# An adjacency-product kernel on one core: the seventh product of layer 0 in the inner level, the bias put into PSUM banks, h normalized in its own tile

## The chip, the cores and the metric

The kernel runs on 1 core of one Trainium2 chip. The metric is the device time of one execution in microseconds (us), as the median of several runs; lower is better. A profiled execution gives, besides its own time, a trace with the start and duration of every instruction. Engines: PE is TensorE (matmuls), PEld its weight loads, DVE VectorE, ACT ScalarE, POOL GpSimd, and SP the engine whose queue issues nearly all DMAs here.

## The reference, cut to what matters

```python
x, adj                                    # (16, 1024, 512), (1024, 1024), float32
# layer 0
h = jnp.maximum(_layernorm(x, axis=-1), 0.0)
y = jnp.einsum('nm,bmd->bnd', adj, h)
x = x + jnp.einsum('bnd,do->bno', y, weight) + bias
# layer 1
h = jnp.maximum(_layernorm(x, axis=-1), 0.0)
# h = h @ W; att = softmax over j of leaky_relu(s1_i + s2_j) * adj
# x = x + elu(att @ h + beta * h)
```

Layer 0 multiplies, for each of 16 batch elements b, the adjacency matrix with h, and the result with a 512 x 512 weight matrix, adds the bias, and adds all to x. Layer 1 has the same two products, with a softmax in between.

## The kernel before

**Two-level products.** Each product of 1024 x 1024 by 1024 x 512 is done with Strassen's scheme in Winograd's form: seven products of blocks (p1 to p7) in place of eight, with sums of blocks on the way in and out (`PRODUCTS`, line 44). Each product writes into PSUM banks of a kind: Y, W or X, two banks each (one for each p, q). `ReadA` (line 125) reads finished banks into SBUF as C11, C12, C21, C22, from which the left operands S1, S2, S4 of the following weight product are made.

**The inner level.** For elements b = 1 to 15, `products_a2` (line 209) runs in layer 0. There p1, p2, p5, p6, p3 and p4 are themselves done by seven smaller products r1 to r7 (`inner_steps`, line 217). One step is two matmuls of 128x256. Step r1 writes y, r5 writes x, r4, r2 and r3 write the banks i0 and i1 of the kind, and r6 and r7 go on adding to y. ScalarE copies y out after r1 and r7 and x after r5; VectorE adds after r6, r7 and r3. Where a product is the first of its kind, x is the unused half of i0; else y and x are banks of their own:

```python
            y = bank(f"{name}_{prod}y")[:, 0:256]
            x = i0[:, 256:512] if first else bank(f"{name}_{prod}x")[:, 0:256]
```

The seventh, p7, is plain: eight matmuls of 128x512 (`plain_steps`, line 276). The products go in pairs whose steps alternate: (p1, p2), (p6, p5), (p3, p7), then p4, whose steps alternate with the first matmuls of the weight product. Each pair has seven turns. For b = 0, `products_a` (line 190) does all seven products plainly.

**The weight product.** `Weighted` (line 337) runs the seven products against the weight blocks into banks po_Y, po_X, po_W; after each, `to_residual` (line 593) adds the bank to the tile xr, which holds x and, from `add_bias` (line 585), the bias.

**What stands beside.** A plan names the work of the other engines after each turn: `after(k)` runs step k (0 to 27 in `products_a2`; `plan_out`, `plan_norm_a`, `plan_bias` and others). Engines keep the order of the program. In `plan_norm_a(b + 1)` the statistics (`Norm.sums`, line 481: two ScalarE passes over 128x512 with a sum, and a small step between) stand at steps 14 to 17 and the Relus (`relu`, line 499) at 18 and 19. `inner_left` (line 424) makes the left sums of an inner product on VectorE, four additions of 128x256. `logits` are VectorE's products with a vector.

**Buffers.** Tiles come from pools: b8 (10), b4 (12), up (7), ld (2), xp (4), b2 (5), and psum, all 8 banks of PSUM. A tile that takes a buffer waits until the last reader of the one before is done; the framework sets the semaphores, and for PSUM by whole bank. x is loaded into ld tiles (`load_x`, line 515) and normalized from there into h (b8). The inner right-hand sums `ext` (line 397) fill up, one b4 and two b2 tiles. A b4 tile `junk` takes results that nobody reads.

Of the kernel before, what the change touches and what calls it, by code (L numbers as in the profile page):

```python
# [34 lines left out]
P = 128  # L35
# [30 lines left out]
def kernel(  # L66
# [29 lines left out]
    psum = ctx.enter_context(tc.tile_pool(name="psum", bufs=8, space=bass.MemoryType.PSUM))  # L96
# [28 lines left out]
    class ReadA:  # L125
# [3 lines left out]
        def __init__(self, name, fork=None):  # L129
            self.name, self.c, self.s, self.s3_now, self.fork = name, {}, {}, True, fork  # L130

# [5 lines left out]
        def __call__(self, prod, p, ps):  # L137
            s = self.s
            if prod == "p1":
                act.copy(self.fork(p) if self.fork else self.block("C11", p), ps)  # L140
            elif prod == "p2" and self.fork:
                act.copy(self.block("C11", p), ps)
            elif prod == "p2":
                c11 = self.block("C11", p)
                add(c11, ps, c11)
            elif prod == "p6":
                act.copy(self.block("C12", p), ps)
            elif prod == "p5":
                act.copy(self.block("C22", p), ps)
            elif prod == "p7":  # L150
                c22 = self.block("C22", p)
                add(c22, ps, c22)
            elif prod == "p3":
                if not s:
                    for k in ("S1", "S2", "S4"):
                        s[k] = b4.tile([P, 2, 512], F32, tag="b4", name=f"{self.name}_{k}")
                c11, c12, c22 = (self.block(n, p) for n in ("C11", "C12", "C22"))
                s1, s2 = s["S1"][:, p, :], s["S2"][:, p, :]
                add(c12, ps, c12)
                add(s1, c12, c22)  # L160
                add(s2, s1, c11, ALU.subtract)
                if self.s3_now:
                    self.s3(p)
            else:
                act.copy(self.block("C21", p), ps)
                self.last(p)
# [23 lines left out]
    def products_a(name, a_blk, b_blk, after, products=PRODUCTS):  # L190
# [7 lines left out]
        read = ReadA(name, fork if products is FORKED else None)  # L198
# [10 lines left out]
    def products_a2(name, a_blk, b_blk, inner, weighted, after):  # L209


        read = ReadA(name)
# [4 lines left out]
        def inner_steps(prod):  # L217
# [5 lines left out]
            if first:  # L223
                banks[kind, 0], banks[kind, 1] = bank(f"{name}_{kind}0"), bank(f"{name}_{kind}1")
            i0, i1 = banks[kind, 0], banks[kind, 1]
            y = bank(f"{name}_{prod}y")[:, 0:256]
            x = i0[:, 256:512] if first else bank(f"{name}_{prod}x")[:, 0:256]
# [13 lines left out]
                "r1": (y, True), "r4": (i0[:, 0:256], first), "r5": (x, not first),  # L241
# [31 lines left out]
            order = ("r1", "r4", "r5") if first else ("r1", "r5", "r4")  # L273
            return [partial(step, r) for r in (*order, "r6", "r2", "r7", "r3")]

        def plain_steps(prod):
            _, an, bn, kind, first, last = by_name[prod]
            if first:
                banks[kind, 0], banks[kind, 1] = bank(f"{name}_{kind}0"), bank(f"{name}_{kind}1")
            return [  # L280
                partial(
                    plain_a, banks[kind, p], p, partial(a_blk, an), partial(b_blk, bn), (k,),
                    first, last,
                )
                for p in range(2) for k in range(HC)
            ]
# [5 lines left out]
        for one, two in (("p1", "p2"), ("p6", "p5")):  # L292
            ones, twos = inner_steps(one), inner_steps(two)
            turns = ones[0:2] + [t for m in range(5) for t in (twos[m], ones[m + 2])] + twos[5:]
            for m in range(7):
                turns[2 * m]()
                turns[2 * m + 1]()
                if m == 0 and k:
                    reads("p2", 0)
                    reads("p2", 1)  # L300
                elif m in (4, 5):
                    reads(one, m - 4)
                elif m == 6 and k:
                    reads(two, 0)
                    reads(two, 1)
                after(k + m)
            k += 7
        inn, pla = inner_steps("p3"), plain_steps("p7")
        turns = [(inn[0], inn[1]), pla[0:2], (inn[2], pla[2]), (inn[3], pla[3]), (inn[4], pla[4])]
        turns += [(inn[5], pla[5]), (inn[6], *pla[6:8])]  # L310
        for m, turn in enumerate(turns):
            for step in turn:
                step()
            if m == 3:
                reads("p7", 0)
            elif m == 5:
                reads("p3", 0)
            elif m == 6:
                reads("p7", 1)
                reads("p3", 1)  # L320
            after(k + m)
        k += 7
# [14 lines left out]
    class Weighted:  # L337
# [4 lines left out]

        def fork(self, kind, q, ps):
# [3 lines left out]
        def steps(self, n, left):  # L347

            prod, _, bn, kind, first, last = self.products[n]

# [34 lines left out]
    def w_sums(w):  # L385
# [9 lines left out]
        "p3": ("S4", "B22"), "p4": ("A22", "T4"),  # L395
# [3 lines left out]
    def inner_right(prod, part):  # L399

        r = adjT[INNER[prod][1]]
        if not exts:
            two = [
                pl.tile([P, 2, 2, 256], F32, tag=tag, name=f"ext_{i}")
                for i, (pl, tag) in enumerate(((up, "up"),) * 7 + ((b4, "b4"),))
            ]
            one = [b2.tile([P, 2, 256], F32, tag="b2", name=f"ext_{i}") for i in (8, 9)]
            ext = [two[i // 2][:, i % 2] for i in range(16)] + one
# [28 lines left out]
    def layer0_a2(b, plan):  # L437
        beside(plan)(-1)

        class Inner(dict):  # L440
# [5 lines left out]
        lefts[b] = products_a2(  # L446
            f"y{b}", lambda n, k: h_blk(b, n)[:, k, :], lambda n, k: adjT[n][:, k, :],
            Inner(), weighted[b], beside(plan),
        )
# [15 lines left out]
    class Norm:  # L465


        def __init__(self, name, src, dst, junk=None):
            self.name, self.src, self.dst, self.junk = name, src, dst, junk
# [11 lines left out]
        def sums(self, k):  # L481
# [5 lines left out]
            junk = self.dst[:, k, :] if self.junk is None else self.junk  # L487
# [11 lines left out]
        def relu(self, c=slice(None)):  # L499
            for k in range(self.n):  # L500
                act.activation(
                    self.dst[:, k, c], self.src[:, k, c], AF.Relu,
# [9 lines left out]
    xs = {}  # L512
    h_norms = {}

    def load_x(b, k, pl=None, tag="ld"):
        t = (pl or ld).tile([P, 2, D], F32, tag=tag, name=f"x_{b}_{k}")
        sp.dma_start(out=t, in_=x[b, ts(k, 2 * P), :].rearrange("(k p) d -> p k d", p=P))
        xs[b, k] = t

    def h_stats(b, k, c=0):  # L520

        if c == 0:
            if k % 2 == 0:
                hs[b, k // 2] = b8.tile([P, HC, D], F32, tag="b8", name=f"h_{b}_{k // 2}")
            dst = hs[b, k // 2][:, ts(k % 2, 2), :]
            h_norms[b, k] = Norm(f"h{b}_{k}", xs.pop((b, k)), dst)
# [40 lines left out]
    def layer0_a(b, plan):  # L567
        beside(plan)(-1)
        lefts[b] = products_a(
            f"y{b}", lambda n, k: h_blk(b, n)[:, k, :], lambda n, k: adjT[n][:, k, :],  # L570
            beside(plan),
# [13 lines left out]
    def add_bias(b, nh, q, oh):  # L585

        t = xrs[b, nh, q][:, :, ts(oh, HD)]
        bias = bias_bc[:, None, ts(oh, HD)].to_broadcast([P, 2, HD])
        pool.tensor_tensor(t, t, bias, op=ALU.add)
# [12 lines left out]
    def layer0_b(b, plan):  # L602
        left = lefts.pop(b)
        if b in weighted:
            weighted.pop(b).rest(1, left, beside(plan))
        else:
            Weighted(f"po{b}", w0_c, partial(to_residual, b), A12_LATE).rest(
                0, left, beside(plan)
            )

    junks = []

    def junk(k):

        if not junks:
            junks.append(b4.tile([P, 2, D], F32, tag="b4", name="junk"))
        return junks[0][:, k, :]
# [7 lines left out]
    class LayerOut:  # L625
# [20 lines left out]
        def stats(self, nh, q, k):  # L646
            xr = xrs[self.b, nh, q]
            if k == 0:
                self.us[nh, q] = xr
                self.norms[nh, q] = Norm(f"u{self.b}_{nh}_{q}", xr, xr, junk(0))  # L650
# [30 lines left out]
    class LateOut(LayerOut):  # L681


        def load(self, g):
# [7 lines left out]
            self.norm = Norm(f"u{self.b}_{g}", self.u[:, 0:1, :], self.u[:, 0:1, :])  # L692
# [308 lines left out]
    for k in range(2):  # L1001
        load_x(0, k, xp, "xp")
# [3 lines left out]
    for k in range(2, 4):  # L1006
        load_x(0, k, xp, "xp")
# [19 lines left out]
    pool.tensor_scalar(bias_bc, bias_bc, -1.0, 1.0, op0=ALU.add, op1=ALU.mult)  # L1027
# [4 lines left out]
    load_x(1, 0)  # L1032
    load_x(1, 1)
# [50 lines left out]
    def plan_first():  # L1084
# [5 lines left out]
            6: [(w_sums, w0_c), (inner_right, "p1", 1), (inner_right, "p2", 0)],  # L1090
            7: [(inner_right, "p2", 1), (inner_right, "p6", 0), (inner_right, "p6", 1)],
            8: [(inner_right, "p5", 0), (inner_right, "p5", 1)], 9: [(inner_right, "p3", 0)],
            10: [(inner_right, "p4", 0)],
# [8 lines left out]
    def at_end(plan):  # L1102

        return merged(*({min(4 + k // 2, 13): v} for k, v in plan.items()))

    def plan_out(o, b):
# [9 lines left out]
            (9, o.logits, 1, 0, 1), (10, inner_left, b, "p3"), (12, o.logits, 0, 1, 0),  # L1116
            (13, o.logits, 0, 1, 1), (15, o.logits, 1, 1, 0), (16, o.logits, 1, 1, 1),
# [5 lines left out]
    def plan_bias(b):  # L1123
        return steps(
            *(
                (k, add_bias, b, *t) for k, t in enumerate((
                    (0, 0, 1), (0, 1, 1), (1, 0, 1), (1, 1, 1), (0, 0, 0), (0, 1, 0), (1, 0, 0),
                    (1, 1, 0),
                ))
            )  # L1130
        )

    def plan_norm_a(b):
        return steps(
            (14, h_stats, b, 0, 0), (15, h_stats, b, 0, 1), (16, h_stats, b, 1, 0),
            (17, h_stats, b, 1, 1), (18, h_relu, b, 0), (19, load_x, b, 2), (19, h_relu, b, 1),
            (20, load_x, b, 3),
        )

    def plan_norm_b(b):  # L1140
        plan = steps(
            (2, h_stats, b, 2, 0), (3, h_stats, b, 2, 1), (4, h_stats, b, 3, 0),
# [3 lines left out]
        if b + 1 < B:  # L1146
            plan = merged(plan, steps((8, load_x, b + 1, 0), (8, load_x, b + 1, 1)))
        return plan
# [52 lines left out]
    for b in range(B):  # L1201
        plans = [plan_out(out_of, b)] if b else []
        plans_b = [plan_bias(b)]
        if b + 1 < B:
            plans.append(plan_norm_a(b + 1))
# [18 lines left out]
        if b == 0:  # L1224
# [3 lines left out]
                    1: [(inner_right, "p3", 1)], 2: [(inner_right, "p4", 1)],  # L1228
# [4 lines left out]
        else:  # L1233
            plan_b = merged(*plans_b)
            plans.append({k: plan_b.pop(i) for k, i in ((23, 0), (26, 1))})
# [74 lines left out]
```

## Time and profile before

| | |
|---|---|
| median of 3 runs | 2278.09 us (2277.12 to 2279.21) |
| the profiled execution, its own time | 2277.24 us |
| its span in the trace | 2275.2 us |
| 0 to 91.25 us: start and element 0 | PE busy 86.09 us |
| 91.25 to 1033.43 us: layer 0, elements 1 to 14 | PE busy 942.18 us |
| 1033.43 to 1100.80 us: layer 0, element 15 | PE busy 64.32 us |
| 1100.80 to 2275.20 us: layer 1 | PE busy 1161.73 us of 1174.40 |

How to read the profile: in a group or timeline line, `out<-in` are the program's tile names without numbers, then come the shapes and how often (x). In a timeline line the first two numbers are the start, counted from the span's start, and the length; `[0.77 <-DVE y_X]` says that the engine was idle for 0.77 us and what ended it. In a line of waits come the total, how many, and the longest. One matmul of the program is two records of the trace in this data type. All engine calls go through one helper, so all lines say L115 and one goes by the tile names: y_p6y is y of p6 in layer 0, y_p6t the SBUF tile that its copies go to, in_p a tile of left sums (its last quarter takes the copy of x), y_Y, y_W, y_X the banks of the kinds, y_C and y_S the blocks C and S, po_ the weight product of layer 0, z_ and pq_ the products of layer 1.

### The profile page before, as it was taken

The numbers are of one execution on the slowest core, as the hardware profiler recorded it, in microseconds if no ns is written. First come the engines' busy times: TensorE is split into PE (matmuls) and PEld (weight loads), VectorE is DVE, ScalarE is ACT, GpSimd is POOL, SyncE is SP. The second block draws the span as 40 slices with busy tenths as digits, with TensorE's granted clock in tenths as the row PEclk, the third lists the DMA queues.
The fourth block names the chain that finished last, engine by engine and source line by source line (L and its number), as shares of the span: only waits on it lengthen the run. The fifth ranks groups of instructions, "written<-read, shape, count | busy, mean of one in ns | idle before, by whom it ended". The sixth has DMA issues, their size and how long they took to land.

```text
span 2275.2 us, 29359 instructions
## 1 busy us (share of the span) xinstructions
PE 2254.3 (99%) x8344; PEld 1578.3 (69%) x8344; DVE 1863.5 (82%) x4101; ACT 1540.7 (68%) x4147; POOL 526.6 (23%) x680
## 2 busy tenths in 40 slices
PE   9999999999999999999999999999999999999998
PEld 5888888888888888887666556654666556665565
DVE  7887787888888888789898888878888887888774
ACT  3666777676677776676476767767776767767753
POOL 1333213233322233221121122201221022201220
PEclk9999999999999999999999999999999999999999
DMA  6344444334444334335535554464545554455441
GB/s 217 121 140 139 140 158 135 139 131 156 131 140 167 130 139 141 112 121 177 198 109 178 169 158 143 156 197 153 166 146 171 171 160 128 131 170 169 135 129 37
DMA packets 194290, 336.00 MB, mean 148 GB/s; under 512 B 78800, under 2 KB 86992, under 8 KB 194128
## 3 DMA queue, kind: packets, MB, share of 16 engines
q1 hardware_dynamic: 193808, 333.61, 45.1%
q8 instruction: 65, 1.06, 0.2%
q14 instruction: 97, 0.79, 0.1%
q10 hardware_dynamic: 320, 0.52, 0.1%
HBM read 228.33 MB, written 109.91 MB: 149 GB/s over the span
## 4 chain that ended last, share of the span: by engine, by line
PE 86%; DVE 5%; DMA 4%; ACT 2%; SPq 1%; issue 1%; POOL 0%; DVEq 0%; ACTq 0%; POOLq 0%
PE z_Y L115 15%; PE y_Y L115 11%; PE po_Y L115 10%; PE pq_Y L115 8%; PE z_X L115 7%; PE po_X L115 5%; PE y_X L115 5%; PE pq_X L115 4%; PE z_W L115 4%; PE y_W L115 3%; PE po_W L115 2%; PE pq_W L115 2%; PE y_p1y L115 2%; PE y_p5y L115 2%; PE y_p6y L115 2%; PE y_p2y L115 2%
## 5 line engine op out<-in xcount | busy, mean ns | idle before, releaser
L115 POOL TENSOR_TENSOR x<-x,r 128x512 f32<-128x512 f32 x120 | 198.9, 1674 | 887.1 <-DVE x L115 272.7
L115 ACT ACTIVATE e<-e,nm 128x256 f32<-128x256 f32 x480 | 237.2, 497 | 139.6 <-DVE nm L115 139.6
L115 DVE CUSTOM_DVE_ANT_0 e<-e,mask 128x256 f32<-128x256 f32 x512 | 226.1, 498 | 107.1 <-DMA mask<-maskd 95.6
L115 PE MATMUL z_Y<-pT,ul_U 128*128 128x512 f32 x512 | 224.9, 592 | 0.0
L115 ACT ACTIVATE e<-s2b,s1b 128x256 f32<-128x256 f32 x512 | 216.5, 501 | 0.0
L115 POOL TENSOR_TENSOR xr<-xr,bias_bc 128x512 f32<-128x512 f32 x128 | 162.1, 1288 | 191.5 <-DVE xr L115 182.1
L115 PE MATMUL po_Y<-w_c,y_C 128*128 128x256 f32 x768 | 188.3, 379 | 0.0
L115 PEld LDWEIGHTS z_Y<-pT,ul_U 128*128 128x128 f32 x512 | 97.3, 190 | 115.6 <-issue 110.5
L115 PE MATMUL pq_Y<-w_c,z_C 128*128 128x256 f32 x768 | 175.0, 380 | 1.9 <-ACT z L115 1.9
L115 DVE CUSTOM_DVE_ANT_0 junk<-xr,v_bc 128x512 f32<-128x512 f32 x240 | 166.0, 692 | 5.2
L115 PEld LDWEIGHTS pq_Y<-w_c,z_C 128*128 128x128 f32 x768 | 145.3, 190 | 30.7 <-issue 7.6
L115 PEld LDWEIGHTS po_Y<-w_c,y_C 128*128 128x128 f32 x768 | 146.0, 190 | 20.2 <-issue 0.5
L115 DVE STREAM_TRANSPOSE pT<-e 128x512 f32<-128x512 f32 x240 | 155.6, 686 | 1.0
L115 PE MATMUL y_Y<-adjT_B,h 128*128 128x512 f32 (+1 forms) x332 | 147.2, 554 | 0.9 <-DVE adjT_B L115 0.9
L115 ACT ACTIVATE h<-x,nb_h,r_h 128x512 f32<-128x512 f32 (+1 forms) x132 | 98.2, 792 | 52.0 <-POOL nb_h L115 52.0
L115 ACT ACTIVATE junk<-xr 128x512 f32<-128x512 f32 x120 | 75.6, 630 | 70.5 <-DVE xr L115 69.9
L115 PE MATMUL po_X<-w_c,y_S 128*128 128x256 f32 x512 | 115.7, 379 | 0.0
L115 PE MATMUL pq_X<-w_c,z_S 128*128 128x256 f32 x512 | 115.6, 379 | 0.0
L115 PE MATMUL z_Y<-pT_T,ul_U 128*128 128x512 f32 x256 | 113.1, 593 | 1.1 <-DVE pT_T L115 1.1
L115 PE MATMUL z_Y<-pT_T,ul_S 128*128 128x512 f32 x256 | 112.5, 592 | 0.0
L115 PE MATMUL z_X<-pT,ul_S 128*128 128x512 f32 x256 | 112.5, 592 | 0.0
L115 PE MATMUL z_W<-pT,ul_U 128*128 128x512 f32 x256 | 112.5, 592 | 0.0
(227 smaller groups left out, 5037.7 us busy)
## 6 DMA issues: line engine op xcount, KB each, us to landing
mask<-maskd SPq DMA_DIRECT2D x128, 512.0 KB
x<-in_x_dram SPq DMA_DIRECT2D x64, 512.0 KB
xr<-in_x_dram SPq DMA_DIRECT2D x256, 128.0 KB
x1d<-xr SPq DMA_DIRECT2D x64, 512.0 KB
ul_U<-ud_U SPq DMA_DIRECT2D x64, 512.0 KB
x<-x1d SPq DMA_DIRECT2D x64, 512.0 KB
out_dram<-x SPq DMA_DIRECT2D x252, 128.0 KB
ud_U<-xr SPq DMA_DIRECT2D x60, 512.0 KB
```

What stands on the lines that cost most here:

```text
L115: return lambda *args, **kwargs: tc.keep_in_program_order(f(*args, **kwargs))
```

## The change

- p7 goes to the inner level too; the third pair is now (p7, p3), run by the same loop as the other two. `plain_steps` goes.
- PSUM is split: `psum` has 6 banks, a new pool `psum_y` 2. In the inner level y and, where the product is not the first of its kind, x are the two halves of one psum_y bank. In p3 r4 now comes ahead of r5.
- The bias is no longer added to xr. `begin` has ScalarE copy a bias row into the Y and X banks of the weight product before the first matmul, which then adds to it. `add_bias` and `plan_bias` go.
- x is loaded straight into h's b8 tile and normalized in place, at other steps of the plan; ld tiles now hold part of `ext`, which grows by p7's three sums.
- `junk` is no tile of its own: each element's S4 tile serves until S4 is written.

```diff
-    psum = ctx.enter_context(tc.tile_pool(name="psum", bufs=8, space=bass.MemoryType.PSUM))
+    psum = ctx.enter_context(tc.tile_pool(name="psum", bufs=6, space=bass.MemoryType.PSUM))
+    psum_y = ctx.enter_context(tc.tile_pool(name="psum_y", bufs=2, space=bass.MemoryType.PSUM))
...
-            y = bank(f"{name}_{prod}y")[:, 0:256]
-            x = i0[:, 256:512] if first else bank(f"{name}_{prod}x")[:, 0:256]
+            yx = psum_y.tile([P, 512], F32, tag="psy", name=f"{name}_{prod}y")
+            y, x = yx[:, 0:256], (i0 if first else yx)[:, 256:512]
...
-                "r1": (y, True), "r4": (i0[:, 0:256], first), "r5": (x, not first),
+                "r1": (y, True), "r4": (i0[:, 0:256], first), "r5": (x, False),
...
-            order = ("r1", "r4", "r5") if first else ("r1", "r5", "r4")
+            late = first or prod == "p3"
+            order = ("r1", "r4", "r5") if late else ("r1", "r5", "r4")
             return [partial(step, r) for r in (*order, "r6", "r2", "r7", "r3")]
...
-        for one, two in (("p1", "p2"), ("p6", "p5")):
+        for one, two in (("p1", "p2"), ("p6", "p5"), ("p7", "p3")):
             ones, twos = inner_steps(one), inner_steps(two)
...
-        inn, pla = inner_steps("p3"), plain_steps("p7")
-        turns = [(inn[0], inn[1]), pla[0:2], (inn[2], pla[2]), (inn[3], pla[3]), (inn[4], pla[4])]
-        turns += [(inn[5], pla[5]), (inn[6], *pla[6:8])]
...
+        def begin(self, kind, row):
+            for q in range(2):
+                b = self.banks[kind, q] = bank(f"{self.name}_{kind}{q}")
+                act.copy(
+                    b.rearrange("p (i o) -> p i o", i=2), row[:, None, :].to_broadcast([P, 2, HD])
+                )
...
         def steps(self, n, left):
             prod, _, bn, kind, first, last = self.products[n]
+            first = first and (kind, 0) not in self.banks
...
-                for i, (pl, tag) in enumerate(((up, "up"),) * 7 + ((b4, "b4"),))
+                for i, (pl, tag) in enumerate(((up, "up"),) * 7 + ((ld, "ld"),) * 2 + ((b4, "b4"),))
...
-    def load_x(b, k, pl=None, tag="ld"):
-        t = (pl or ld).tile([P, 2, D], F32, tag=tag, name=f"x_{b}_{k}")
+    def load_x(b, k):
+        if k % 2 == 0:
+            hs[b, k // 2] = b8.tile([P, HC, D], F32, tag="b8", name=f"h_{b}_{k // 2}")
+        t = hs[b, k // 2][:, ts(k % 2, 2), :]
         sp.dma_start(out=t, in_=x[b, ts(k, 2 * P), :].rearrange("(k p) d -> p k d", p=P))
...
+    def new_junk(b):
+        junks.append(b4.tile([P, 2, D], F32, tag="b4", name=f"y{b}_S4"))
...
+    b_lo, b_hi = bias_bc[:, 0:HD], bias_bc[:, HD:D]
+    pool.tensor_tensor(b_hi, b_hi, b_lo, op=ALU.subtract)
+    pool.tensor_scalar(b_lo, b_lo, -1.0, 1.0, op0=ALU.add, op1=ALU.mult)
...
-            (9, o.logits, 1, 0, 1), (10, inner_left, b, "p3"), (12, o.logits, 0, 1, 0),
-            (13, o.logits, 0, 1, 1), (15, o.logits, 1, 1, 0), (16, o.logits, 1, 1, 1),
+            (9, o.logits, 1, 0, 1), (10, inner_left, b, "p7"), (12, o.logits, 0, 1, 0),
+            (13, inner_left, b, "p3"), (14, o.logits, 0, 1, 1), (20, begin, b, "Y"),
+            (24, begin, b, "X"), (15, o.logits, 1, 1, 0), (16, o.logits, 1, 1, 1),
...
-            (17, h_stats, b, 1, 1), (18, h_relu, b, 0), (19, load_x, b, 2), (19, h_relu, b, 1),
-            (20, load_x, b, 3),
+            (17, h_stats, b, 1, 1), (18, h_relu, b, 0), (19, h_relu, b, 1), (22, load_x, b, 2),
+            (22, load_x, b, 3),
...
+                plans.append(steps((-1, load_x, b + 1, 0), (-1, load_x, b + 1, 1)))
```

In element 0, `begin` stands at steps 12 and 13, and what stands beside its end is one step earlier (`at_end`, 3 + k // 2 in place of 4 + k // 2).

## The prediction

> **What bounds the kernel now.** I read the page first (busy shares, chain), then the waits of TensorE, then busy time by stage, then the timeline of one batch element of layer 0, engine by engine.
>
> ```profile
> span 2275.2 us, 29359 instructions
> PE 2254.3 (99%) x8344; PEld 1578.3 (69%) x8344; DVE 1863.5 (82%) x4101; ACT 1540.7 (68%) x4147; POOL 526.6 (23%) x680
> ...
> PE pq_Y L115 <- ACT z L115: 1.9, 3, 0.9
> PE y_p4y L115 <- DVE y_p4t L115: 1.6, 1, 1.6
> ...
> 91.25:1033.43 942.18, 942.18 (x4145) 787.52 (x4144) 783.55 (x1679) 666.44 (x1714) 273.97 (x462) 1.00 0.41 138
> ```
>
> TensorE is busy 99% of the span. Its longest waits for others are near 2 us in total. In the last line (start:end, length, then busy time of PE, weight loads, DVE, ACT, POOL, the granted clock, the DMA share, GB/s) it has no idle time in fourteen elements of layer 0 (b = 1 to 14): 942.18 / 14 = 67.3 us each. So a matmul saved is worth its time, and so is every wait put before one. The waits matter, so I show one element (b = 11), first TensorE:
>
> ```profile
> 776.34 1.03 PE L115 MATMUL y_p6y<-adjT_T,hS 128*128 128x256 f32 x4
> 777.20 1.03 PE L115 MATMUL y_p6x<-ext,in_p 128*128 128x256 f32 x4
> ...
> 788.42 1.03 PE L115 MATMUL y_p3y<-adjT_B,hS 128*128 128x256 f32 x4
> 789.29 1.03 PE L115 MATMUL y_p3x<-ext,in_p 128*128 128x256 f32 x4
> 790.15 1.88 PE L115 MATMUL y_Y<-adjT_B,h 128*128 128x512 f32 x4
> ...
> 801.33 1.03 PE L115 MATMUL y_p4y<-adjT_T,h 128*128 128x256 f32 x4
> ```
>
> One step of the inner level (two matmuls, four records) starts every 0.863 us, and its result is complete 1.03 us after its start. The r1 step (into y) is followed at once by r5 (into x, a bank of its own). Then ScalarE and VectorE:
>
> ```profile
> 777.40 0.37 ACT L115 COPY y_p6t<-y_p6y 128x256 f32<-128x256 f32 x1
> ...
> 789.24 0.38 ACT L115 COPY y_p5t<-y_p5y 128x256 f32<-128x256 f32 x1
> 790.38 1.18 ACT L115 COPY y_C<-y_X 128x512 f32<-128x512 f32 x2 [0.77 <-DVE y_X L115]
> 791.46 0.38 ACT L115 COPY y_p3t<-y_p3y 128x256 f32<-128x256 f32 x1
> 791.72 0.39 ACT L115 COPY in_p<-y_p3x 128x256 f32<-128x256 f32 x1
> ...
> 800.59 0.42 DVE L115 TENSOR_TENSOR y_p3t<-y_p3y,in_p 128x256 f32<-128x256 f32 x1 [2.57 <-ACT y_p3t L115]
> ...
> 806.60 0.69 DVE L115 TENSOR_TENSOR y_S<-y_S,y_C 128x512 f32<-128x512 f32 x1
> 807.21 0.41 DVE L115 TENSOR_TENSOR y_p4t<-y_p4y,in_p 128x256 f32<-128x256 f32 x1
> ```
>
> See how late ScalarE copies y out: after p6's r1 the copy ends at 777.77, when r5 has run for 0.57 us; after p3's r1 it ends at 791.84, 2.55 us after r5 began. The fifteen elements agree: 0.57 for p6, 2.54 or 2.55 for p3 (2.75 in the last). In the kernel before this costs nothing, as x and y are different banks.
>
> [...] hS<-h,h took 1.40 us at 823.73, beside a bias addition on GpSimd, and 0.68 us at 828.18, with none. [...] the trace shows next to no difference: 128x512 copies take 563 (pq_W<-pq_Y) and 586 ns (z_W<-z_Y) into PSUM, 575 (z_C<-z_Y) and 586 (y_C<-y_X) into SBUF.
>
> **The change, part by part.** The saving: p7 as eight plain matmuls is 8 x 0.859 = 6.87 us (1.72 for two in the timeline); as seven steps 7 x 0.863 = 6.04. The pair p3 and p7 took 801.33 - 788.42 = 12.91 us and will be issued in 14 x 0.863 = 12.08: 0.83 us less an element, 15 x 0.83 = 12.4 us in all (b = 0 is plain in both).
>
> The price: with psum_y, y and x of p6, p7, p3 and p4 are halves of one bank. In the instruction order of the changed program, r5 of p6, p7 and p4 now waits for ScalarE's copy of y, and r6 for its copy of x. From the end of a copy to TensorE's next start are 0.05 us (z<-pq_Y ends at 1240.91, TensorE starts at 1240.96), and the first records after a wait run 0.11 us longer (three after the wait at 1067.93 take 0.92; 0.379 + 2 x 0.216 = 0.81). For each wait I add 0.16.
> 1. p6, r5: 0.57 + 0.16 = 0.73 us.
> 2. p7, r5: p7's r1 takes the place of p3's, and ScalarE's queue ahead of it is the same: p6's copy, VectorE's sums, two Relus, p5's copy, two copies y_C. 2.55, less 0.1 since wait 1 moves TensorE but ScalarE was already 0.1 behind there: 2.45 + 0.16 = 2.6 us.
> 3. p3, r6: its r5 now comes two steps before r6. Counted from p7's r5: ScalarE begins the copy of p7's x at 1.18 (1.03 + 0.11 + 0.04) and is free 0.26 later, at 1.44. Then follow a stretch of statistics of 1.74 us (791.98 to 793.72), p3's first copy (0.26), two stretches (2 x 1.7), and only then the copy of p3's x (0.37): it ends at 7.21, while r6 is due at 7 x 0.863 + 0.11 = 6.15. 1.06 + 0.16 = 1.2 us.
> 4. p4, r5: one matmul of 0.43 lies between r1 and r5. ScalarE is still at four Relus (2.8), p3's last copy, and the two new bias copies (0.48 each); this leaves r5 0.2 + 0.11 late: 0.3 us.
> 5. p4, r7 waits for VectorE's sum after r6. Before, that sum ended at 807.62, 0.6 us ahead of r7. VectorE gets for p7: 4 x 0.34 (left sums), 2 x 0.42 and 2 x 0.70 = 3.6 us an element, of which some 2 us stand just ahead of the chain from p3's last sum to S2 (800.59 to 807.21, 6.6 us; 6.0 without one y_C sum that moves ahead). Laid after the waits above, the sum ends 0.8 us after r7 is due: 0.8 + 0.16 = 0.95 us.
> Together 5.78 us, less 0.83: 4.95 us an element, 15 x 4.95 = 74 us.
>
> Bias: eight additions on GpSimd an element (1288 ns) go; four ScalarE copies of 128x512 come (4 x 0.48 = 1.9 us of issue). ScalarE has 666.4 us busy in those 942, so the sum of it fits; what does not is in wait 4. The copies for X wait for VectorE to read the X banks, some 4 us before po_X begins: nothing. GpSimd's relief makes VectorE faster in the weight products, which TensorE hides anyway: nothing, below nothing at most where VectorE was the last to come, and there it was not.
> In place, and the loads: x for element b+1 is loaded at step -1 and 22 in place of 8, 19 and 20, each after the last reader of that tile. SP issues the later pair (512 KB each) after load_res and before the mask load and the keeps; from p7's last step to the first statistics are some 10 us, against 9.2 before (issued 800.33, read 809.57). Nothing taken; 2 us an element at worst if it lands late, and ScalarE gets back 2.27 us that its second Relu waited for GpSimd. The scratch in S4's tile has the same writers in the same order on ScalarE and VectorE: nothing.
> Six banks for the rest: in layer 1 I put each new bank wait against the times of before, and none ends after TensorE needs it: nothing. At the start sixteen transposes share fewer banks; copies of adjT end up to 1.99 us after TensorE began there, of which 0.95 was idle before: 1 us, once.
>
> Sum: 2277.24 (the profiled execution; its span is 2275.2) + 74 + 1 = 2352 us. The median of the runs is 2278.09, 0.85 higher, well within the error of this.
>
> **Rivals.** (a) Only waits 1 and 2 bite: TensorE's own delay lets ScalarE and VectorE catch up, so 3 to 5 vanish. 0.73 + 2.6 - 0.83 = 2.5, x 15 = 38, + 1: 2316 us. For it: both queues have idle time (ScalarE 5.24 us before 809.30). Against: that idle time lies after p4, not before. (b) Waits pile up: copies that come late delay VectorE's chain up to po_X, or the next element begins late because h lands late; 2 to 4 us more an element: 2382 to 2412. For it: the last element already waited 1.5 and 1.6 us on VectorE. (c) Faster: r5 is held for less than 0.83 us an element in all, because ScalarE is ahead at p6, p7 and p4 once the work around is re-ordered. It decides at r5 of p7: the 2.55 must fall to nothing. Then 2277 - 12 + 1 = 2266 us. Against: the queue ahead of that copy is the same, and r5 follows r1 without a gap. (d) No change: waits of 0.83 us an element, 2278 us; it needs a coincidence.
>
> **How the numbers follow.** Forecast 68%, (a) 13%, (b) 13%, (c) 4%, (d) 2%. The bounds of waits 3 to 5 (none, or twice: 0 to 4.9 against 2.45) give 2316 to 2389; the range 2314 to 2389 holds the forecast, (a) and the lower part of (b). No change means within 0.2% (4.6 us), about what a measurement of this kernel can tell: faster 0.04, same 0.02, slower 0.94.
>
> **What would show it.** In the profile after: TensorE idle before y_p7y of some 2.6 us an element, put down to ACT y_p7t, and 0.7 before y_p6y on ACT y_p6t; then smaller ones before y_p3y (ACT in_p) and y_p4y (ACT, DVE); elements of 72 us in place of 67.3; no new idle time in layer 1. Wrong if TensorE has no gap at r5, or if the gaps stand in layer 1 or at po_Y, po_X.

## The result, and the profile after

| | before | after |
|---|---|---|
| median of the runs | 2278.09 us (2275.66 to 2279.61) | 2360.54 us (2357.92 to 2362.26) |
| ratio, 95% interval | | 1.0361 (1.0346 to 1.0376) |
| span of the profiled execution | 2275.2 us | 2359.8 us |
| elements 1 to 14 of layer 0, each | 67.30 us | 72.80 us |
| element 15, to the first matmul of layer 1 | 70.88 us | 76.78 us |
| layer 1, from there to the end | 1170.8 us | 1173.1 us |

The kernel became 3.6% slower. 77 of the 84.6 us that the span grew by lie in elements 1 to 14 (14 x 5.50), 5.9 in element 15, 2.3 in layer 1; the start became 0.5 us shorter. (Layer 1 is counted here from its first matmul, at 1104.39 us in before; the border at 1100.80 in the table of before lay a little ahead of it.)

First the page of after (span, busy time by engine, the chain that ended last, by engine):

```profile
span 2359.8 us, 29840 instructions
PE 2277.9 (97%) x8524; PEld 1620.7 (69%) x8524; DVE 1899.5 (80%) x4225; ACT 1592.8 (67%) x4256; POOL 367.6 (16%) x553
...
PE 60%; ACT 16%; DVE 14%; DMA 5%; issue 3%; SPq 2%; DVEq 0%; POOL 0%; ACTq 0%; POOLq 0%
```

TensorE fell from 99% to 97%, and in the chain ScalarE went from 2% to 16% and VectorE from 5% to 14%: TensorE now waits for them many times. GpSimd is relieved (526.6 to 367.6 us), and nothing got faster by it as a whole. The waits of TensorE in after (what waited, line, what ended it; us in total, how many, the longest):

```profile
PE y_p7y L118 <- ACT y_p7t L118: 36.6, 15, 2.4
PE y_p4y L118 <- DVE y_p4t L118: 7.6, 14, 0.5
PE y_p6y L118 <- ACT y_p6t L118: 6.9, 15, 0.5
PE y_p3y L118 <- ACT in_p L118: 6.5, 8, 1.0
PE y_p4y L118 <- ACT y_p4t L118: 3.6, 1, 3.6
```

The first line is r5 of p7, held by ScalarE's copy of y in each of the 15 elements. These idle times run from the modelled end of the step before; from start to start TensorE is 0.16 us later still. They make some 61 us; the rest shows in the timeline of element 11 around p7's r5, ScalarE first, then TensorE:

```profile
845.26 1.18 ACT L118 COPY y_C<-y_X 128x512 f32<-128x512 f32 x2 [0.77 <-DVE y_X L118]
846.34 0.38 ACT L118 COPY y_p7t<-y_p7y 128x256 f32<-128x256 f32 x1
```

```profile
843.31 1.03 PE L118 MATMUL y_p7y<-adjT_B,h 128*128 128x256 f32 x4
846.77 2.07 PE L118 MATMUL y_p7y<-ext,in_p 128*128 128x256 f32 x4 [2.44 <-ACT y_p7t L118]
848.64 1.64 PE L118 MATMUL y_p3y<-adjT_B,hS 128*128 128x256 f32 x4
```

p7's r1 is complete at 844.34, but ScalarE first waits for VectorE and copies both X banks of p5; its copy of y ends at 846.72, and TensorE starts 0.05 us later. The step then takes 2.07 us, and the one after it 1.64, in place of 1.03: the records come 426 to 428 ns apart in place of 216. Nine of the fourteen elements have such a stretch of 5 to 7 half-speed records; the last section shows when they come.

The table by stage is the yardstick for all runs below. Each number is from the start of TensorE's first record of a stage to that of the next, as a mean over elements 1 to 14, from the traces.

| kernel | p6, p5 | p7, p3 | p4 | element | element 15 | median of runs |
|---|---|---|---|---|---|---|
| before | 12.09 | 12.91 | 9.50 | 67.30 | 70.88 | 2278.09 |
| after | 12.82 | 16.50 | 10.68 | 72.80 | 76.78 | 2360.54 |
| before, bank shared | 12.82 | 16.32 | 9.79 | 71.73 | 72.51 | 2345.18 |
| after, own banks | 12.09 | 12.09 | 14.09 | 71.07 | 78.02 | 2336.65 |
| after, own banks, bias on GpSimd | 12.09 | 12.09 | 16.37 | 73.52 | 78.42 | 2373.30 |
| after, bias on GpSimd | 12.82 | 16.35 | 11.66 | 73.74 | 78.64 | 2373.49 |
| after, r4 ahead of r5 | 12.09 | 14.82 | 10.67 | 70.38 | 77.36 | 2328.83 |
| after, X copies late | 12.82 | 15.12 | 10.68 | 71.42 | 76.44 | 2341.13 |
| both of these | 12.09 | 14.56 | 10.67 | 70.12 | 77.33 | 2324.38 |
| after, statistics moved | 12.82 | 15.26 | 10.67 | 71.55 | 76.69 | 2343.17 |
| rearranged | 12.09 | 12.09 | 9.79 | 66.79 | 76.83 | 2281.28 |
| rearranged, repaired | 12.09 | 12.09 | 9.79 | 66.77 | 74.02 | 2273.72 |
| the same, r7 ahead of r3 | 12.09 | 12.09 | 10.70 | 67.68 | 72.94 | 2288.68 |
| the same, bias on GpSimd | 12.09 | 12.09 | 9.79 | 67.22 | 72.77 | 2277.47 |

(p1, p2) takes 12.09 us and the weight product after p4 20.72 in nearly all of them ((p1, p2): 12.53 in the last, 12.18 and 12.19 in the other two with the bias on GpSimd). The kernel before was run again beside each group: 2278.44, 2279.37, 2278.46 and 2280.32 us.

### The profile page after: what moved, and what is told of

It is laid out like the page before. It is cut to its first block, busy times and chain, and to the rows that moved or that the text cites. A ratio compares the mean times of both kernels' runs of the same rounds, so it can differ in the third digit from the quotient of the medians.

```text
span 2359.8 us, 29840 instructions
## 1 busy us (share of the span) xinstructions
PE 2277.9 (97%) x8524; PEld 1620.7 (69%) x8524; DVE 1899.5 (80%) x4225; ACT 1592.8 (67%) x4256; POOL 367.6 (16%) x553
## 4 chain that ended last, share of the span: by engine, by line
PE 60%; ACT 16%; DVE 14%; DMA 5%; issue 3%; SPq 2%; DVEq 0%; POOL 0%; ACTq 0%; POOLq 0%
PE z_Y L118 13%; PE po_Y L118 8%; PE pq_Y L118 8%; ACT y_S L118 6%; PE z_X L118 6%; PE po_X L118 5%; PE pq_X L118 4%; ACT xr L118 4%; PE z_W L118 3%; PE y_Y L118 3%; PE po_W L118 2%; PE pq_W L118 2%; DMA mask<-maskd 2%; DVE e L118 2%; SPq L118 2%
## 5 line engine op out<-in xcount | busy, mean ns | idle before, releaser
L118 DVE CUSTOM_DVE_ANT_0 e<-e,mask 128x256 f32<-128x256 f32 x512 | 215.5, 478 | 109.8 <-DMA mask<-maskd 96.1
L118 DVE CUSTOM_DVE_ANT_0 y_S<-xr,v_bc 128x512 f32<-128x512 f32 x240 | 165.4, 689 | 7.5 <-ACT xr L118 2.8
L118 ACT ACTIVATE y_S<-xr 128x512 f32<-128x512 f32 x120 | 75.5, 629 | 105.2 <-DVE xr L118 104.7
L118 DVE TENSOR_TENSOR xr<-po_Y,xr 128x512 f32<-128x512 f32 x128 | 87.6, 685 | 35.6 <-PE po_Y L118 35.6
L118 PE MATMUL z_X<-pT_T,ul_S 128*128 128x512 f32 x256 | 112.5, 592 | 0.0
L118 PEld LDWEIGHTS pq_X<-w_c,z_S 128*128 128x128 f32 x512 | 97.4, 190 | 13.1
```

Source lines behind the costliest of these rows:

```text
L118: return lambda *args, **kwargs: tc.keep_in_program_order(f(*args, **kwargs))
```

## The experiments

### The shared bank alone, put into the kernel before

```diff
-    psum = ... bufs=8
+    psum = ... bufs=6
+    psum_y = ... bufs=2
-            y = bank(f"{name}_{prod}y")[:, 0:256]
-            x = i0[:, 256:512] if first else bank(f"{name}_{prod}x")[:, 0:256]
+            yx = psum_y.tile([P, 512], F32, tag="psy", name=f"{name}_{prod}y")
+            y, x = yx[:, 0:256], (i0 if first else yx)[:, 256:512]
```

> The kernel before, with only the banks of the change: six banks and two, y and x of one inner product as halves of one bank (p7 stays plain, p3 keeps r1, r5, r4). Theory, the shared bank alone makes the loss: gaps of 0.6 to 0.75 us before r5 of p6, about 2.6 us before r5 of p3 (followed by half-speed records worth 1.5 us), and up to 0.4 at p4: 4 to 5.5 us in each of 15 elements, 2335 to 2362 us. Rival, the loss needs p7 in the inner level or the moved bias: within 15 us of 2278.

Measured: 2345.18 us, ratio 1.0290 (1.0273 to 1.0307). The longest wait of TensorE in this run:

```profile
PE y_p3y L116 <- ACT y_p3t L116: 36.7, 15, 2.6
```

With p7 still plain, p3's r5 waits as p7's r5 does in after, 36.7 against 36.6 us in total: who comes first in the third pair waits for ScalarE. So the shared bank, without anything else, makes 67 us of loss. It is enough; the next run asks whether it is the only cause.

### Own banks for y and x, put into the kernel after

```diff
-    psum = ... bufs=6
-    psum_y = ... bufs=2
+    psum = ... bufs=8
-            yx = psum_y.tile([P, 512], F32, tag="psy", name=f"{name}_{prod}y")
-            y, x = yx[:, 0:256], (i0 if first else yx)[:, 256:512]
+            y = bank(f"{name}_{prod}y")[:, 0:256]
+            x = i0[:, 256:512] if first else bank(f"{name}_{prod}x")[:, 0:256]
```

> The kernel after, with one edit: one pool of eight banks again, and y and x of each inner product in banks of their own (p7 stays in the inner level, all other parts of the change stay). Theory, the shared bank: TensorE's gaps before r5 of p6, p7 and p4 and before r6 of p3 go, and with them the half-speed records after the gap at p7; what stays is at most the wait of p4's r7 on VectorE and a new one at p4's r5, 0 to 1.2 us an element. Elements of 66.5 to 68 us in place of 72.8, 2266 to 2290 us in all. Rival, the seventh inner product itself (more work on VectorE and ScalarE, seven steps where one plain product had slack): elements stay above 70 us and the time above 2320 us.

Measured: 2336.65 us, ratio 1.0256 (1.0238 to 1.0274). (This kernel leaves part of the bias out of its output, so it tests the price of the shared banks and is no replacement for them; the work issued is the same.) The expected gain did not come: only 24 of the 82 us were given back. The table says where they went: the pairs lost nothing any more (12.09 and 12.09), and p4 took 14.09 us in place of 10.68. The waits of TensorE, and the timeline at the start of p4 in element 14, ScalarE and VectorE:

```profile
PE po_Y L117 <- ACT po_Y L117: 26.7, 14, 1.9
PE y_p4x L117 <- DVE y_p3t L117: 13.3, 15, 2.8
```

```profile
1049.36 2.93 ACT L117 ACTIVATE h<-h,nb_h,r_h 128x512 f32<-128x512 f32 x4
...
1052.44 1.10 ACT L117 COPY po_Y<-bias_bc 128x512 f32<-128x512 f32 x2
```

```profile
1054.08 0.41 DVE L117 TENSOR_TENSOR y_p3t<-y_p3y,in_p 128x256 f32<-128x256 f32 x1
```

ScalarE puts the bias into po_Y only at 1052.44, after the Relus of the next h (2.93 us); and p4's x takes the bank of p3's y, which VectorE reads last, at 1054.08. TensorE, no longer stopped in the pair, arrives at p4 before ScalarE and VectorE have done what p7's steps and the early bias copies gave them. The rival's figures held: above 70 us an element (71.07), above 2320 us in all. Yet the shared bank alone made 67 us of loss in the run before. Either is enough for a loss, and they cover each other: what TensorE does not lose in the pair, it loses at p4. That the second cause is a lack of time on ScalarE or VectorE, as the rival had it, does not follow; the rearranged kernel below decides that.

### Own banks, and the bias on GpSimd

The edit is the diff above together with that of the next run. GpSimd adds the bias into xr again, as in the kernel before.

> Own banks for y and x as in the first run, and the bias back on GpSimd, so that no bank is held early for the bias. The run with own banks alone lost 2.07 us an element at po_Y, behind ScalarE's copy of the bias, and 0.94 at p4's r5, behind VectorE's sum of p3. Theory A (eight banks are too few for own y and x banks and banks held early for the bias; the wait at po_Y is the bank's): po_Y's wait and the half-speed records go, p4's r5 keeps some 0.9 us and p4's r7 comes later by up to 1 us because GpSimd slows VectorE: 2280 to 2305 us. Theory B (po_Y waits because ScalarE is late with its copies, whatever the bank): the wait moves to another step of the weight product or of p4, 2320 us or more.

Measured: 2373.30 us, ratio 1.0407 (1.0386 to 1.0428). The wait at po_Y went, as theory A said, but p4 became longer still, 16.37 us: the outcome is theory B's, though not by ScalarE. The timeline of VectorE in element 14, and of GpSimd beside it:

```profile
1080.45 0.42 DVE L117 TENSOR_TENSOR y_p7t<-y_p7y,in_p 128x256 f32<-128x256 f32 x1 [1.54 <-ACT y_p7t L117]
...
1082.26 0.87 DVE L117 TENSOR_TENSOR in_p<-h 128x256 f32<-128x256 f32 x1
1083.16 1.37 DVE L117 TENSOR_TENSOR in_p<-in_p,h 128x256 f32<-128x256 f32 x1
...
1092.21 0.42 DVE L117 TENSOR_TENSOR y_p4t<-y_p4y,in_p 128x256 f32<-128x256 f32 x1
```

```profile
1081.56 2.68 POOL L117 TENSOR_TENSOR xr<-xr,bias_bc 128x512 f32<-128x512 f32 x2
```

VectorE has no pause from 1080.45 to 1092.63, and p4's r7 waits for the sum at the end of that chain, 3.63 us, with half-speed records behind it in all fourteen elements. Two of its sums took 0.87 and 1.37 us beside GpSimd's bias additions; elsewhere they take 0.42. This is the second limit: a row of VectorE's additions without a pause between p7's r7 and p4's r7, 12.2 us here and, undisturbed, 10.8 in after (857.50 to 868.27).

### The bias on GpSimd, shared banks kept

```diff
-            12: [(begin, 0, "Y")], 13: [(begin, 0, "X")],
...
-            (13, inner_left, b, "p3"), (14, o.logits, 0, 1, 1), (20, begin, b, "Y"),
-            (24, begin, b, "X"), (15, o.logits, 1, 1, 0), (16, o.logits, 1, 1, 1),
+            (13, inner_left, b, "p3"), (14, o.logits, 0, 1, 1), (15, o.logits, 1, 1, 0),
+            (16, o.logits, 1, 1, 1),
...
-        plans_b = []
+        plans_b = [plan_bias(b)]
```

> The kernel after, with the bias added by GpSimd into the tile xr as in the kernel before and no ScalarE copies into the Y and X banks; everything else stays. Theory (bias costs TensorE next to nothing, only part of the wait at p4's r5): 0 to 0.5 us an element less, 2352 to 2362 us. Rival, ScalarE's four copies stand before p4's copies and hold p4's steps r5 to r7: 1 us or more an element less, 2345 us or lower. Other side: GpSimd's additions slow VectorE's sums (1.40 in place of 0.68 us beside one), and p4's r7 comes later: up to 1 us an element more, 2375 us.

Measured: 2373.49 us, ratio 1.0416 (1.0400 to 1.0432): the other side of the three. p4 grew from 10.68 to 11.66 us, and the wait at its r7 on VectorE from 7.6 to 22.4 us in total. In element 11 one of VectorE's left sums for p4 took 1.47 us from 869.04 on, beside two of GpSimd's additions (867.72 to 870.23), in place of 0.41 in after, and the chain from p7's r7 to p4's r7 took 11.8 us in place of 10.8. Moving the bias to ScalarE, by itself, is therefore worth 13 us of gain in the kernel after.

### r4 ahead of r5 in every product

```diff
-            late = first or prod == "p3"
+            late = True
```

> The kernel after, with r4 put ahead of r5 in every inner product; y and x still share a bank. r5 then comes one step (two with the pair's turns, 0.86 to 1.73 us) later behind r1. Theory, r5 held by ScalarE's copy of y: the gap at p6 goes (it was 0.63 us), that at p7 shrinks from 2.6 us to about 0.9 us, that at p4 goes; and if the half-speed records come only after a long stop, they go too. 2.5 to 5 us less an element, less what moves to r6 (up to 1 us): 2290 to 2325 us. Rival, the wait is set by VectorE or by work further ahead and only moves to another step: the time stays within 10 us of the kernel after.

Measured: 2328.83 us, ratio 1.0222 (1.0207 to 1.0238), 4 us above the range given. The gap at p6 went; at p7's r5 0.92 us stayed (start to start), no half-speed records followed in elements 1 to 14, but 0.4 us came at p7's r6 and 1.1 us stood at p3's r6 in every element, and p4's r7 kept its wait.

### p5's X banks copied behind the copy of p7's y

```diff
-                if m == 0 and k == 7:
-                    reads("p2", 0)
-                    reads("p2", 1)
+                if m == 0 and k:
+                    reads("p2" if k == 7 else "p5", 0)
+                    reads("p2" if k == 7 else "p5", 1)
...
-                elif m == 6 and k:
+                elif m == 6 and k == 14:
```

> The kernel after, with one edit: ScalarE's copies of p5's X banks (y_C<-y_X) are issued behind the first turn of (p7, p3), so behind the copy of p7's y, not ahead of it. Theory (the 2.6 us at p7's r5 are ScalarE's queue, above all those two copies and their wait for VectorE): the wait before p7's r5 falls from 2.6 to 0.6 to 0.8 us as at p6, no half-speed records follow it, and p3's r6 has its 1.2 us in every element: 1.6 to 2.5 us less an element, 2322 to 2338 us. Rival (the wait at p7 is VectorE's or only moves on, as p3's steps wait for the same X banks): less than 0.7 us an element, 2350 us or more.

Measured: 2341.13 us, ratio 1.0266 (1.0244 to 1.0287). The waits of this run:

```profile
PE y_p3y L118 <- ACT in_p L118: 25.4, 15, 1.8
PE y_p7y L118 <- ACT y_p7t L118: 7.3, 15, 0.5
```

The wait at p7's r5 fell from 36.6 to 7.3 us, with two copies on ScalarE issued later and nothing else changed; so those 2.6 us were a place in ScalarE's queue. But p3's r6 rose from 6.5 to 25.4: TensorE came there earlier and met the same statistics. The gain was 1.4 us an element, less than I gave.

### Both of these

The two diffs above together.

> The edit of the late copies and r4 ahead of r5 in every product, together; y and x share a bank. Theory: no wait is left at r5 of p6 and p7; left are r6 of p7 (0.4), r6 of p3 (1.1) behind ScalarE's statistics and r7 of p4 (0.76) behind VectorE: about 2.5 us an element above 66.5, 69.0, in all 2300 to 2318 us. Rival (the waits add up to the same total because ScalarE's and VectorE's work in these two pairs is the bound): within 8 us of the run with r4 ahead of r5 alone, 2321 us or more.

Measured: 2324.38 us, ratio 1.0191 (1.0167 to 1.0215): the rival's figure. p7's r5 has no wait left, but its r6 comes 1.16 us late (0.40 without the late X copies) and p3's r6 still 1.1: what one wait gave up, the next one took, as long as the statistics stood where they were.

### The statistics moved, alone

(Those of element 1, which stand beside element 0, keep their old steps.)

```diff
-            (14, h_stats, b, 0, 0), (15, h_stats, b, 0, 1), (16, h_stats, b, 1, 0),
-            (17, h_stats, b, 1, 1), (18, h_relu, b, 0), (19, h_relu, b, 1), (22, load_x, b, 2),
+            (17, h_stats, b, 0, 0), (18, h_stats, b, 0, 1), (21, h_stats, b, 1, 0),
+            (24, h_stats, b, 1, 1), (26, h_relu, b, 0), (27, h_relu, b, 1), (22, load_x, b, 2),
```

> The kernel after, with one edit: the statistics of the next h at steps 17, 18, 21 and 24 (Relus 26, 27) in place of 14 to 17 (18, 19), elements 2 to 15. The stop of 2.6 us at p7's r5 stays. In the kernel after the pair (p7, p3) took 16.09 us in five elements of fourteen, with 1.2 us at p3's r6 and no half-speed records, and 16.5 to 17.0 in nine, with half-speed records and little or no wait at p3's r6. Theory (p3's r6 is held by ScalarE's statistics; the half-speed records, worth 1.47 us, come from the stop at p7 and partly stand in for that wait): the pair falls into two groups, 14.7 to 14.9 us without half-speed records and 16.1 to 16.4 with, and the run gets 0.6 to 1.2 us an element shorter, 2342 to 2352 us. Rival (p3's r6 waits for something else, or what it gives back is lost at p4's r7 behind VectorE's chain): within 5 us of 2360.

Measured: 2343.17 us, ratio 1.0275 (1.0258 to 1.0293), 17 us less than after. The wait at p3's r6 is gone from the list of waits, and the pair falls into two groups: 14.79 to 14.80 us in ten of elements 1 to 14, 16.28 to 16.48 in the four with half-speed records. TensorE after the same stop of 2.44 us, in element 1 of this run, without them:

```profile
120.20 1.13 PE L118 MATMUL y_p7y<-ext,in_p 128*128 128x256 f32 x4 [2.44 <-ACT y_p7t L118]
121.17 1.03 PE L118 MATMUL y_p3y<-adjT_B,hS 128*128 128x256 f32 x4
```

### Rearranged: r4 late, X copies late, statistics moved, and r3 ahead of r7 in p4

The three diffs above together, and:

```diff
-            return [partial(step, r) for r in (*order, "r6", "r2", "r7", "r3")]
+            ends = ("r3", "r7") if prod == "p4" else ("r7", "r3")
+            return [partial(step, r) for r in (*order, "r6", "r2", *ends)]
...
-                read.last(m - 5)
+                read.last(6 - m)
```

> As the run before it, and two more edits against the waits that would be left: the statistics of the next h at steps 17, 18, 21 and 24 (their Relus at 26 and 27) in place of 14 to 17 (18, 19), so that no copy of x stands behind them, and in p4 r3 ahead of r7. Theory (each wait is a place in the queue of ScalarE or VectorE, and none is the lack of time on them): elements of 66.5 to 67.3 us, 2264 to 2282 us. Rival (VectorE or ScalarE lacks time in the pair (p7, p3) and p4, the wait moves to the weight product or to the next element): elements of 68 us or more, 2290 us or more.

Measured: 2281.28 us, ratio 1.0004 (0.9994 to 1.0014). (In it the moved statistics write their scratch into element 0's S4 tile after S4 was made, so that element 0 of layer 0 comes out wrong; the work is the same.) Elements took 66.79 us, as the theory said, with y and x still in one bank and p7 in the inner level. What was left was lost at the ends: a start of 95.4 us and an element 15 of 76.8.

### Rearranged and repaired

The next kernel leaves element 1's statistics at their old steps and moves element 15's exponentials:

```diff
-        11: "R0", 12: "R1", 14: "B E0", 15: "V0 R2", 16: "E1", 17: "V1 E2", 18: "V2", 20: "b R3",
-        22: "E3", 23: "V3 R4", 24: "S", 25: "E4", 26: "V4 R5",
+        11: "R0", 12: "R1", 14: "B E0", 15: "V0 R2", 16: "E1", 17: "V1", 18: "R3", 20: "E2", 21: "V2 b R4",
+        24: "E3 V3 S", 25: "R5", 26: "E4", 27: "V4",
```

> The rearranged kernel, with two repairs: element 1's statistics and Relus, which stand beside element 0, stay at their old steps, and in element 15 the first softmax's exponentials of layer 1 (E2, E3, E4, which ScalarE waits for DMA with) come behind the copies of y and x that TensorE waits for. The run before had elements of 66.77 us, a start of 95.4 in place of 91.3 us, and an element 15 of 76.8 us. Theory (what was lost there is again ScalarE's queue ahead of a copy): start 91 to 92, element 15 at 67 to 70 us, in all 2262 to 2272 us, below the kernel before. Rival (element 15 is bound by the DMA that brings er, the wait moves on into layer 1): 2274 us or more.

Measured: 2273.72 us, ratio 0.9976 (0.9969 to 0.9983) with 18 runs of it and 30 of before: faster than both kernels, by 4.7 us (0.2%) and 86.8 us, though 2 us above the range I gave. Its layer 0 from element 1 to 14, in the same view as the last line shown of before (start:end, length, busy time of PE, weight loads, DVE, ACT, POOL, clock, DMA share, GB/s):

```profile
91.00:1025.83 934.83, 934.41 (x4314) 818.12 (x4313) 810.48 (x1791) 716.58 (x1810) 141.67 (x351) 1.00 0.42 141
```

ScalarE has 716.6 us of work there in 934.8, VectorE 810.5: neither lacks time for p7 in the inner level. In these fourteen elements each wait of after was a matter of order. Four places in it were changed together: one of them, r3 and r7, is taken back alone below; whether each of the other three is needed beside the rest was not tried. The loads, h in its own tile and the scratch in S4's were not tried apart either, but this kernel has them all. Element 15 still takes 74.0 us (70.9 before, 67 to 70 expected), and why was not tried further.

### The repaired kernel with r7 ahead of r3 again

The diff of r3 and r7 is taken back, all else stays.

> The same with r7 ahead of r3 in p4 again, as in the kernel after. Theory (p4's r7 is held by VectorE's chain from p7's last sum to the sum after p4's r6, about 12 us of additions without a pause, and not by the bank): a wait on VectorE comes back at p4's r7, 0.8 to 1.6 us an element since TensorE no longer stops earlier, 12 to 24 us more than with r3 ahead: 2275 to 2292 us. Rival (that chain was late only because ScalarE's copies were, which the new order has mended): within 4 us of the kernel with r3 ahead.

Measured: 2288.68 us, ratio 1.0049 (1.0034 to 1.0065). p4 took 10.70 in place of 9.79 us: VectorE's chain holds r7 by 0.9 us an element even with ScalarE's copies in time. The rival is out.

### The repaired kernel with the bias on GpSimd

The diff of the bias on GpSimd, put into the repaired kernel.

> The kernel of the first of these three, with the bias added by GpSimd into xr again. In the run with own banks and the bias on GpSimd, two of VectorE's left sums for p4 took 0.87 and 1.37 us beside such an addition, in place of 0.42 each. Theory (GpSimd's additions lengthen VectorE's chain by about 1.4 us, which reaches TensorE only where that chain is late): 0.3 to 1.5 us an element more, 5 to 22 us more than with the bias on ScalarE. Rival (r3 ahead of r7 gives the chain enough room, and ScalarE is spared four copies): within 3 us, or faster.

Measured: 2277.47 us, ratio 0.9995 (0.9987 to 1.0003), 3.7 us above the kernel with the bias on ScalarE, between what the two theories gave. With r3 ahead of r7, p4 shows nothing of it (9.79); (p1, p2) takes 0.44 us more, and element 15 1.25 us less.

## Why the prediction was right, and where it was off

The direction, the place and the mechanism were right; 2352 stood against 2360.5. Step by step:

- **The saving of 0.83 us.** With nothing in the way, the pair takes 12.09 in place of 12.91 us: 0.82.
- **Wait 1, 0.73.** (p6, p5) took 12.82 in place of 12.09: 0.73.
- **Wait 2, 2.6, and wait 3, 1.2.** The moved statistics tell them apart: 14.80 - 12.09 = 2.71 for wait 2, and the five elements of after that have no half-speed records took 16.09, so 1.29 for wait 3. Each is 0.1 short; for wait 2 that is the 0.1 that I took off: TensorE started 2.60 us late, and 2.55 + 0.16 is 2.71. That the queue ahead of p7's y is the cause is shown by the run with late X copies.
- **Waits 4 and 5, 0.3 and 0.95.** p4 grew by 1.18 us; I had 1.25 for both. From start to start r5 came 0.26 and r7 0.70 us late, and slower records added 0.10 each: 0.36 and 0.81. That wait 5 is VectorE's chain is shown by the run with r7 ahead of r3 again.
- **The term that was missing.** I gave every wait 0.11 us of slower records after it. After the stop at p7 nine of fourteen elements had a half-speed stretch as well. It partly stands in for wait 3 (ScalarE gets on with its statistics meanwhile), so the pair took 16.47 to 17.04 us there, and 16.50 on the mean: 0.41 us an element, about 6 us in all. This and the two times 0.1 make 5.50 in place of 4.95 us an element: 14 x 0.55 = 7.7 of the 9.6 us by which the span grew more than my sum.
- **Element 15** I had counted like the others. It lost 5.9 us, but elsewhere: p4 took 16.20 us there, against 11.33 before. ScalarE's copy of p4's y stood idle for 4.03 us until VectorE was done with y_Y, and TensorE 3.64 for that copy, with half-speed records behind it. In the rearranged kernel, moving the first softmax's exponentials, with VectorE's turns after them, brought p4 from 17.40 to 11.25 us in that element (though the weight product behind it then took 24.81 in place of 20.72); for after itself that cause is argued, not shown.
- **The start** I put at +1 us; it was -0.5. **Layer 1** I put at nothing; it was +2.3 us. No run takes these apart, and neither is clear of noise: in the seven traces whose layer 1 is that of after, it took 1169.45 to 1175.85 us (1170.80 before), and in the five of these that also share its start, that took 90.75 to 91.83 (91.25 before).
- **The bias: GpSimd's relief "nothing".** This step failed. I looked for GpSimd's additions only beside the weight products, where TensorE hides VectorE. They also run beside p4's left sums, in the middle of VectorE's chain, and without the relief the kernel after takes 13 us more. That the sum did not suffer is luck: wait 5 was worked out with undisturbed sums, one every 0.34 us, and it is the relief that keeps them so.
- **The rivals.** Rival (a) supposed that TensorE's own delay lets the others catch up. Between waits that is what the runs show, with the sign turned round: take one wait away, and the next grows. But in after all five stood, wait 3 in full only in the elements without a half-speed stretch. Rival (c) needed r5 of p7 to be held for next to nothing. The place where it was to be decided, r5 of p7, was well chosen: the rearranged kernel has no wait there, and repaired it is the one that is faster.

## What to carry to other kernels

Before two results are put into one PSUM bank, read from the timeline how late the first of them is copied out: that lateness, not the length of the copy, was TensorE's wait ahead of the second here (2.6 us, for a copy of 0.38). Waits behind in-order queues cover one another, so the gain of taking one away is not its length in the list (with late X copies the waits at p7's r5 fell by 29.3 us, and the time by 19.4); it is found only by asking which is late next, and here the seventh product paid after four places in the order were mended together. Mend the order of a queue before spending banks: in elements 1 to 14 the shared bank cost 0.3 us each at most (p4, 9.79 against 9.50) once ScalarE's copies were issued ahead of its statistics and long copies.

## What the runs showed of the hardware that was not expected

The half-speed stretches: records of 128x256 come 426 to 428 ns apart in place of 216, five to seven in a row, after a stop of 2.44 us at p7's r5 (TensorE 2.60 us late, from start to start). The same stop brought them in nine of fourteen elements of after, in eight with the bias on GpSimd and in four with the statistics moved, where the pair took 1.5 to 1.7 us more for it; at p3's r5, with the bank shared in the kernel before, in six. Single stops that delayed TensorE by up to 1.96 us (p3's r6 with late X copies, in all of them) brought none in those fourteen elements; with own banks, two stops 1.5 us apart (1.90 and 0.77 us idle) brought them in twelve of fourteen.

The trace also holds the clock that TensorE was granted, and it shows what these stretches are. Around the stop in element 11 of after (start:end, length, busy time of PE, clock, DMA share, GB/s):

```profile
843.04:846.45 3.41, 1.29 (x6) 1.00 0.54 189
846.45:849.86 3.41, 3.09 (x7) 0.50 0.52 144
```

In the traces the clock falls to half for 3.41 us at a time (6.83 where two such stretches join; only the last one, at the end of the trace, has another length), and within a trace these stretches begin whole multiples of 3.41 us apart. So each trace can be cut into such windows. In nine of after's elements one window held 1.97 us or more of the stop as idle time, and the next ran at half; in the other five the stop lay across the border of two windows, and neither held more than 1.93. In all fourteen traces together, from 20 us on to 15 us before the end, a window at full clock with under 1.7 us of idle time was never followed by one at half clock, and one with over 2.0 us always was; between these both occur. With late X copies no window of those fourteen elements held more than 1.80 us.

So a window need not be idle as a whole: 1.97 us of 3.41 were enough in after. What counted in these runs is therefore how much of a stop fell into one window.
